# Value projection from rows instead of window columns, with its result sent through DRAM, and the bias product moved to the front of the projection

## The chip, the core and the metric

The kernel runs on one core of one Trainium2 chip. The metric is device time in microseconds (us), from the first to the last instruction and the few microseconds around them. Before the change three runs gave 4484.2, 4484.65 and 4484.88 us; the median is 4484.65 us.

A core has five engines that run side by side, each through its own list of instructions in order: TensorE (PE in the profile; PEld is its weight load), VectorE (DVE), ScalarE (ACT), GpSimd (POOL) and SyncE (SP), which here issues nearly all DMA transfers. Where one engine needs another's result, it waits on a semaphore.

## What is computed

The input is an image batch of shape 2 x 128 x 256 x 256 (batch, channel, row, column) in float32. One layer has two halves. The first is windowed attention with a halo: windows of 8 x 8 pixels ask, windows of 12 x 12 pixels answer, 4 heads of 32 channels. A fixed mask leaves, for each query, only keys of one parity of row and column. The second is a mixture of 8 experts, of which each pixel uses the best 2. Cut to what matters:

```
def conv(x):                        # x is normalised over the 128 channels
    q, k, v = split(W_qkv @ x)      # three 1x1 projections
    q = windows of 8x8 of q;  k, v = windows of 12x12 of k, v (zero padded)
    attn = softmax(q * SCALE @ k.T + rel_pos_emb(q * SCALE) + FIXED_MASK)
    return W_out @ (attn @ v)

def ffn(t):                         # t is normalised over the 128 channels
    p = softmax(t @ router_w);  top 2 of 8, weights scaled to sum 1
    return sum over the two of p_e * (t @ expert_w[e] + expert_b[e])

x = x + conv(ln(x));  x = x + ffn(ln(x))
```

## The kernel before

**Strips and planes.** The image is cut into 64 strips of 8 rows (two batch entries of 32). Because of the mask a query sees only pixels of its own row and column parity, so each strip falls into 4 planes (2 row parities x 2 column parities) of 4 rows by 128 columns. There are 256 planes, counted by `n`; `i, pl = divmod(n, 4)` gives the strip and the plane. In a plane a window has 4 x 4 queries and 6 x 6 keys. Two neighbouring windows are taken together: a pair has a patch of 6 rows by 10 columns, 60 places, padded to 64 (`KR, KC, NK, SLOT`). A plane has 16 pairs, two of which share one 128-row tile.

**The normalised rows.** `xn` (two buffers, one per strip parity) holds the normalised rows of a strip with its halo, channels on the partitions, with a zero column on both sides. `ln1` (L272) writes one row of `xn` per iteration on GpSimd; it needs the broadcast factor `rb`, which comes back from DRAM. `halo` (L246) copies the shared row on GpSimd, once in four iterations.

**Columns and values.** `columns` (L331) copies, on GpSimd, the new rows of `xn` into `xcol`: for each pair of windows the 64 places of its patch stand side by side. `place` (L251) gives a row's place in the ring of 6 rows, and `runs` (L255) groups rows whose places follow one another. `xcol` has one buffer per plane index `pl`, so that only new rows (4 of 6, as a rule) are copied. In `project`, `values` (L366) then runs 4 products of 128 x 128 by 128 x 128 (L369) with 128 columns of `xcol` as the weights, into one PSUM tile, and ScalarE copies that into `vv` (L376). It is called twice per plane: `values(0)` at the head of `project`, `values(4)` at its end. So the value of a pixel that lies in several patches is computed once for each patch.

**The other projections.** `pu` (L384) is the product for the relative position bias; VectorE transposes it into `uT` (L386), and `shift` makes two copies (L349) and one more transpose, `au` (L354). `pk` (L396) is the key projection from whole rows of `xn`; ScalarE spreads it into `kcol` (L407, L414). `pq` (L418) is the query projection; ScalarE copies it into `qs` (L420).

**PSUM.** `pvv`, `pu`, `pk`, `pq`, `plt`, `plg` and `po` all take their place from one pool of three buffers, `ps_mm`, in the order in which they are asked for. A tile can be written once the tile three before it has been read for the last time. Before the change the order in an iteration is `pvv`, `pu`, `pk`, `pq`, `plt`, `pvv`, `plg`, `po`.

**Attention.** `scores` (L448, L465) needs `au`, `kcol` and `qs`; ScalarE's Exp gives `pT` (L473). `attend` sums the weights with `ones` (L486) and multiplies with the values (L496); VectorE transposes the sums (`sT`, L506), inverts them (L508), spreads them (`rT`, L511) and scales the output (`o`, L516). `out_project` (L524) and the sum into `xt` (L529) end the attention of a plane.

**Experts.** For each row pair there are 8 gate tiles `gb`, fetched from DRAM by broadcast (L661). `times` (L677) multiplies the centred input `xs` by a gate into `xe`: VectorE does e = 0, 1, 2, 3, 4, 6, GpSimd e = 5, 7. `product` (L686) accumulates the 8 expert products in `acc`; `end` adds `acc` to `xt` (L692), and `store` writes it out.

**The order of the work** is written by hand: inside the main loop (L779 to L867) each engine keeps the order in which the lines are issued. Generators (`score`, `attn`, `ahead`, `norm` and others) are advanced by `next`. Iteration `n` runs the scores of plane `n`, then `ahead`, which is `project(n + 1)`, then expert products 4, 6, 7, 5 of the row before, the attention of plane `n`, expert products 0, 1, 2, the output projection and expert product 3. On VectorE the routing (L587 to L619) and the transpose of the gates, `gT` (L625), come ahead of `uT`; then come `shift`, `xs` (L671), six `times`, L692, L506 to L516, the transpose `plg` (L563), and `rstd`. On GpSimd a one-column copy, `behind` (L681), waits for VectorE's `xe` number 6; then follow `times(5)`, `ln1`, `halo`, `times(7)` and `columns`. PE's code is padded with empty instructions (L793) so that each iteration starts at the same place in a code block of 256.

**rstd** (L218) makes the reciprocal deviations from `plg`, which lies in PSUM:

```
mean, sq = (p4[:, :, E + 2 * k0 + j : E + 2 * k1 : 2].rearrange("p t k -> p k t") for j in range(2))
nc.vector.tensor_copy(r, mean)                                                  # L228
nc.vector.tensor_tensor(u, r, r, ALU.mult)                                      # L229
nc.vector.scalar_tensor_tensor(u, u, -1.0, sq, ALU.mult, ALU.add)               # L230
nc.vector.scalar_tensor_tensor(u, u, 0.0, epsc[:, k0:k1], ALU.max, ALU.add)     # L231
nc.scalar.activation(r, u, AF.Ln, scale=4.0)                                    # L232
```

`mean` and `sq` are views of PSUM; `r`, `u` and `epsc` lie in SBUF.

Of the kernel before, what the change touches and what calls it, by code (L numbers as in the profile page):

```python
# [11 lines left out]
F32 = mybir.dt.float32  # L12
AF = mybir.ActivationFunctionType
ALU = mybir.AluOpType
# [3 lines left out]
P = 128  # L18
# [33 lines left out]
def kernel(  # L52
# [42 lines left out]
    def ctile(shape, name):  # L95
        return const.tile(shape, F32, tag=name, name=name)
# [98 lines left out]
    nc.tensor.matmul(pr[:, :P], lhsT=wall[:, 0, :], rhs=relbd, start=True, stop=True)  # L195
    nc.vector.tensor_copy(wrel, pr[:, :P])

    xn, xcol, kcol = [], [], []
    for i in range(2):
        xn.append(ctile([P, 2, 2, KR, PC + 2], f"xn{i}"))  # L200
        nc.gpsimd.memset(xn[i][:, :, :, :, 0 : PC + 2 : PC + 1], 0.0)
    for i in range(4):
        xcol.append(ctile([P, HP, 2, SLOT], f"xcol{i}"))
        kcol.append(ctile([P, NP, SLOT], f"kcol{i}"))
        nc.gpsimd.memset(xcol[i][:, :, :, NK:], 0.0)
        nc.gpsimd.memset(kcol[i][:, :, NK:], 0.0)
        nc.gpsimd.memset(kcol[i][:, 0, 0:NK:KC], 0.0)
        nc.gpsimd.memset(kcol[i][:, NP - 1, KC - 1 : NK : KC], 0.0)
# [9 lines left out]
    def rstd(p4, k0, k1, name):  # L218

        u, r = (
            small.tile([P, 2, NT], F32, tag=v, name=f"{v}_{name}")[:, k0:k1] for v in ("u", "r")
        )
        mean, sq = (
            p4[:, :, E + 2 * k0 + j : E + 2 * k1 : 2].rearrange("p t k -> p k t") for j in range(2)
        )
        nc.vector.tensor_copy(r, mean)  # L228
        nc.vector.tensor_tensor(u, r, r, ALU.mult)  # L229
        nc.vector.scalar_tensor_tensor(u, u, -1.0, sq, ALU.mult, ALU.add)  # L230
        nc.vector.scalar_tensor_tensor(u, u, 0.0, epsc[:, k0:k1], ALU.max, ALU.add)  # L231
        nc.scalar.activation(r, u, AF.Ln, scale=4.0)  # L232
        nc.scalar.activation(r, r, AF.Exp, scale=-0.5)
        nc.vector.scalar_tensor_tensor(u, u, -4.0, r, ALU.mult, ALU.mult)
        nc.vector.tensor_tensor(u, u, r, ALU.mult)
        return r, u

    def ln_rows(i):

        s = strips[i][1]  # L240
        return range(1 if s == 0 else 2, KR - 1 if s == NS - 1 else KR)
# [13 lines left out]
    def runs(i, rows):  # L255

        out = []
        for k in rows:
            if out and place(i, k) == out[-1][1] + out[-1][2]:
                out[-1][2] += 1  # L260
            else:
                out.append([k, place(i, k), 1])
        return out
# [59 lines left out]
            ln1(i, k, pb, nc.vector)  # L323
        yield

    def columns(n):

        i, pl = divmod(n, 4)
        for k, at, m in runs(i, ln_rows(i)):
            for half in range(2):  # L330
                nc.gpsimd.tensor_copy(  # L331
                    xcol[pl][:, :, half, at * KC : (at + m) * KC].rearrange(
                        "p t (r c) -> p t r c", c=KC
                    ),
                    windows(xn[i % 2][:, pl // 2, pl % 2, k : k + m], half * HP, HP),
                )
        for k, s in ((0, 0), (KR - 1, NS - 1)):
            if strips[i][1] == s:
                c0 = place(i, k) * KC
                nc.gpsimd.memset(xcol[pl][:, :, :, c0 : c0 + KC], 0.0)  # L340
                nc.gpsimd.memset(kcol[pl][:, :, c0 : c0 + KC], 0.0)

    def shift(uT, n, state):

# [12 lines left out]
    def project(n, state):  # L357

        i, pl = divmod(n, 4)
        xp = xn[i % 2][:, pl // 2, pl % 2]  # L360
        inner = xp[:, 1 : 1 + PR, 1 : PC + 1]
        xl, kk = xcol[pl], kcol[pl]

        vv = work.tile([P, HP, P], F32, tag="vv", name=f"vv{n}")

        def values(t0):  # L366
            pv = mm_tile(f"pvv{n}_{t0}")
            for t in range(4):
                nc.tensor.matmul(  # L369
                    pv[:, t * P : (t + 1) * P],  # L370
                    lhsT=xl[:, t0 + t].rearrange("p a k -> p (a k)"),
                    rhs=wv,
                    start=True,
                    stop=True,
                )
            nc.scalar.copy(vv[:, t0 : t0 + 4, :].rearrange("p t c -> p (t c)"), pv)  # L376

        values(0)
        yield

        pu = mm_tile(f"pu{n}")
        nc.tensor.matmul(pu, lhsT=wrel, rhs=inner, start=True, stop=True)  # L384
        uT = work.tile([P, PR, 4, 32], F32, tag="uT", name=f"uT{n}", bufs=1)
        nc.vector.transpose(uT, pu.rearrange("p (a m s) -> p a s m", a=PR, s=4))  # L386
        state["shift"] = lambda: shift(uT, n, state)
        yield

        rows = list(ln_rows(i))  # L390
        for part in (rows[-4:], rows[:-4]):
            if not part:
                continue
            pk = mm_tile(f"pk{n}_{part[0]}")
            m = len(part)
            nc.tensor.matmul(  # L396
                pk[:, : m * PC],
                lhsT=wk,
                rhs=xp[:, part[0] : part[0] + m, 1 : PC + 1],
                start=True,  # L400
                stop=True,
            )
            pk3 = pk[:, : m * PC].rearrange("p (r c) -> p r c", r=m)
            for k, at, m in runs(i, part):
                new = pk3[:, k - part[0] : k - part[0] + m]
                places = kk[:, :, at * KC : (at + m) * KC].rearrange("p t (r c) -> p t r c", c=KC)
                nc.scalar.copy(places[:, 1 : NP - 1], windows(new[:, :, KC - 3 :], 0, NP - 2))  # L407

                ends = [places[:, 0, :, 1:], new[:, :, 0 : KC - 1]]
                for j, step in enumerate(((NP - 1) * SLOT - 1, PC - KC + 1)):  # L410
                    dims = [list(d) for d in ends[j].unsqueeze(1).ap]
                    dims[1] = [step, 2]
                    ends[j] = bass.AP(ends[j].tensor, ends[j].offset, dims)
                nc.scalar.copy(*ends)  # L414
        yield

        pq = mm_tile(f"pq{n}")
        nc.tensor.matmul(pq, lhsT=wq, rhs=inner, start=True, stop=True)  # L418
        qs = work.tile([P, 2 * NP, PR, 4], F32, tag="qs", name=f"qs{n}")
        nc.scalar.copy(  # L420
            qs.rearrange("p m a s -> p a m s"), pq.rearrange("p (a m s) -> p a m s", a=PR, s=4)
        )
        yield

        values(4)
        state.update(qs=qs, kk=kk, vv=vv)
        yield

    def windows(rows, n0, count):
# [315 lines left out]
            next(part)  # L745
    if len(strips) > 1:
        halo(1)
    columns(0)
    states = {0: {}}
    for _ in project(0, states[0]):  # L750
        pass
    states[0]["shift"]()
    if n_planes > 1:
        columns(1)

# [20 lines left out]
    with tc.manual_schedule(engines={ET.PE, ET.DVE, ET.Activation, ET.Pool, ET.SP}):  # L778
        for n in range(n_planes + 7):  # L779
# [32 lines left out]
            next(ahead, None)  # L812
            if n + 1 < n_planes:
                states[n + 1]["shift"]()
            next(ahead, None)
            next(ahead, None)
            for e in (4, 6, 7, 5):
# [26 lines left out]
            new.fetch(3, dve)  # L844
            while to_store:
                store(*to_store.pop())
            next(ahead, None)
            ex.product(0)
            made = next(norm, None)
# [8 lines left out]
                halo(i + 2)  # L858
            nxt.times(7, pool)
            if n + 2 < n_planes:  # L860
                columns(n + 2)
            next(outp, None)
            ex.product(3)
            next(outp, None)
# [61 lines left out]
```

The softmax here doesn't subtract the row's maximum and nothing guards it: scores larger than these inputs give would overflow.

## Time and profile before

| What | Value |
|---|---|
| three runs | 4484.2, 4484.65, 4484.88 us |
| span of the profiled execution | 4480.1 us (the median run stands 4.55 us above it) |
| mean granted clock of TensorE | 0.997 |
| a usual iteration (from one uT to the next) | 17.16 us |
| ScalarE's and GpSimd's share of the span | 33% and 29% |
| transfer of one gate tile, issue to landing | 4.0 us median, 256 KB |
| write of the gates to DRAM, issue to landing | 3.0 us median, 16 KB |
| transfers issued per iteration | 8 gb, 1 sb, 1 rb, 2 gd, 1 xt, 1 output |

No separate time is listed for the profiled execution; its span is set beside the median of the runs. The page says for every engine how long it was busy, and for the costliest lines how long one instruction took ("mean ns of one"), how long the engine sat idle just before it, and what ended that idle time. A float32 product on PE shows as two instructions; L369's x4096 is 2048 products. The timeline gives start and duration of instructions; overlapping neighbours on PE are pipelined, so the cost of a step is read from one start to the next.

### The profile page before, as it was taken

The numbers are of one execution on the slowest core, as the hardware profiler recorded it, in microseconds if no ns is written. First come the engines' busy times: TensorE is split into PE (matmuls) and PEld (weight loads), VectorE is DVE, ScalarE is ACT, GpSimd is POOL, SyncE is SP. The second block draws the span as 40 slices with busy tenths as digits, with TensorE's granted clock in tenths as the row PEclk, the third lists the DMA queues.
The fourth block names the chain that finished last, engine by engine and source line by source line (L and its number), as shares of the span: only waits on it lengthen the run. The fifth ranks groups of instructions, "written<-read, shape, count | busy, mean of one in ns | idle before, by whom it ended". The sixth has DMA issues, their size and how long they took to land. (4 is left out here: it accounts for less than half of the span.)

```text
span 4480.1 us, 224632 instructions
## 1 busy us (share of the span) xinstructions
PE 4422.6 (99%) x96321; PEld 2683.3 (60%) x96321; DVE 3996.2 (89%) x11850; ACT 1467.7 (33%) x4022; POOL 1317.7 (29%) x1815
## 2 busy tenths in 40 slices
PE   7999999999999999999999999999999999999997
PEld 5666666666666666666666666666666666666653
DVE  5899999999899999998989999999999999989887
ACT  3333333333333333333333333333333333333321
POOL 1232323232323233232323232323232323232321
PEclk9999999999999999999999999999999999999999
DMA  2565666566656666666666566666665666566655
GB/s 83 174 191 185 192 185 192 186 191 185 193 184 192 185 191 187 189 188 188 189 187 189 187 190 185 193 183 193 184 193 185 192 185 192 186 191 186 190 164 186
DMA packets 519284, 828.12 MB, mean 185 GB/s; under 512 B 124186, under 2 KB 125850, under 8 KB 518298
## 3 DMA queue, kind: packets, MB, share of 16 engines
q1 hardware_dynamic: 517568, 813.46, 58.3%
q8 instruction: 769, 12.60, 1.1%
q14 instruction: 217, 1.78, 0.2%
q10 hardware_dynamic: 730, 0.29, 0.0%
HBM read 737.95 MB, written 75.56 MB: 182 GB/s over the span
## 5 line engine op out<-in xcount | busy, mean ns | idle before, releaser
L686 PE MATMUL acc<-xe,ew 128*128 128x512 f32 x4096 | 1889.0, 594 | 19.6 <-DVE gb L660 18.8
L686 PEld LDWEIGHTS acc<-xe,ew 128*128 128x128 f32 x4096 | 758.8, 190 | 885.7 <-issue 861.8
L677 DVE TENSOR_TENSOR xe<-xs,gb 128x512 f32<-128x512 f32 x1536 | 950.9, 687 | 10.2 <-PE acc L686 0.7
L681 POOL COPY last<-xe 128x1 f32<-128x1 f32 x256 | 47.9, 187 | 3060.8 <-DVE gb L660 3054.6
L376 ACT COPY vv<-pvv 128x512 f32<-128x512 f32 x512 | 299.8, 586 | 1395.7 <-PE pvv L369 1379.6
L677 POOL TENSOR_TENSOR xe<-xs,gb 128x512 f32<-128x512 f32 x512 | 650.8, 1272 | 5.9 <-PE att L496 2.5
L369 PE MATMUL pvv<-wt,xcol 128*128 128x128 f32 x4096 | 594.3, 288 | 2.5 <-POOL xcol L331 1.5
L369 PEld LDWEIGHTS pvv<-wt,xcol 128*128 128x128 f32 x4096 | 496.4, 191 | 64.8 <-issue 51.8
L272 POOL TENSOR_TENSOR xn<-xt,rb 128x512 f32<-128x512 f32 x249 | 375.0, 1506 | 66.5 <-DMA rb<-gd 55.9
L465 PE MATMUL att<-qs,kcol 32*64 32x32 f32 x32768 | 392.4, 226 | 0.8 <-issue 0.7
L465 PEld LDWEIGHTS att<-qs,kcol 32*64 32x64 f32 x32768 | 391.0, 130 | 1.0 <-issue 1.0
L496 PEld LDWEIGHTS att<-pT,vv 64*32 64x32 f32 x32768 | 348.0, 105 | 39.4 <-issue 2.5
L496 PE MATMUL att<-pT,vv 64*32 64x32 f32 x32768 | 343.2, 200 | 2.3 <-issue 2.3
L473 ACT ACTIVATE pT<-att 128x1024 f32<-128x1024 f32 x256 | 261.9, 1023 | 243.1 <-PE att L465 239.7
L548 ACT ACTIVATE sq<-xt 128x512 f32<-128x512 f32 x505 | 292.7, 631 | 0.0
L354 DVE STREAM_TRANSPOSE au<-auT 128x512 f32<-128x512 f32 x256 | 269.2, 1052 | 9.0
L524 PE MATMUL po<-o,wt 128*128 128x512 f32 x512 | 262.0, 593 | 6.1 <-DVE o L516 3.2
L384 PE MATMUL pu<-xn,wrel 128*128 128x512 f32 x512 | 262.5, 594 | 0.0
L407 ACT COPY kcol<-pk 128x560 f32<-128x560 f32 (+2 forms) x344 | 174.1, 506 | 268.2 <-PE pk L396 265.3
L418 PE MATMUL pq<-xn,wt 128*128 128x512 f32 x512 | 262.0, 593 | 0.0
L396 PE MATMUL pk<-xn,wt 128*128 128x512 f32 (+2 forms) x528 | 261.0, 578 | 0.0
L386 DVE STREAM_TRANSPOSE uT<-pu 128x512 f32<-128x512 f32 x256 | 182.8, 714 | 78.0 <-PE pu L384 77.0
(2697 smaller groups left out, 5243.8 us busy)
## 6 DMA issues: line engine op xcount, KB each, us to landing
gb<-gd SPq DMA_DIRECT2D x2048, 256.0 KB, 4.0
xt<-in_x_dram SPq DMA_DIRECT2D x256, 256.0 KB, 4.9
sb<-gd SPq DMA_DIRECT2D x256, 256.0 KB, 3.5
out_dram<-xt SPq DMA_DIRECT2D x256, 256.0 KB, 4.2
rb<-gd SPq DMA_DIRECT2D x249, 256.0 KB, 3.3
gd<-gT SPq DMA_DIRECT2D x516, 16.0 KB, 3.0
ew<-in_L_ffn_expert_w_dram SPq DMA_DIRECT2D x1, 512.0 KB, 5.0
eb<-in_L_ffn_expert_b_dram SPq DMA_DIRECT2D x1, 512.0 KB, 5.7
```

The lines of the kernel that those rows point to most:

```text
L272: eng.tensor_tensor(xn[i % 2][:, :, :, k, 1 : PC + 1], ln1_src(i, k).rearrange("p (y j x) -> p y x j", y=2, x=2), rb.rearrange("p (y j x) ...
L354: nc.vector.transpose(au.rearrange("p m a s -> p a s m"), auT[n % 2])
L369: nc.tensor.matmul(pv[:, t * P : (t + 1) * P], lhsT=xl[:, t0 + t].rearrange("p a k -> p (a k)"), rhs=wv, start=True, stop=True,)
L376: nc.scalar.copy(vv[:, t0 : t0 + 4, :].rearrange("p t c -> p (t c)"), pv)
L384: nc.tensor.matmul(pu, lhsT=wrel, rhs=inner, start=True, stop=True)
L418: nc.tensor.matmul(pq, lhsT=wq, rhs=inner, start=True, stop=True)
L465: nc.tensor.matmul(sc[rows, h, 32 * t : 32 * t + 32], lhsT=kk[hp, half * HP + t, :], rhs=qs[hp, m0 : m0 + 2].rearrange("p m a s -> p (m a ...
L496: nc.tensor.matmul(av[hp, half, 32 * t : 32 * t + 32], lhsT=vv[rows, t, hp], rhs=pT[rows, h, 32 * t : 32 * t + 32], start=True, stop=True,)
L524: nc.tensor.matmul(po, lhsT=wo, rhs=state["o"].rearrange("p f z -> p (f z)"), start=True, stop=True)
L548: nc.scalar.activation(sq, src, AF.Square)
L677: eng.tensor_tensor(self.xe[e], self.xs, self.gb.pop(e), ALU.mult)
L686: nc.tensor.matmul(self.acc, lhsT=ew[:, e, :], rhs=self.xe.pop(e), start=(e == 0), stop=not self.xe)
```

## The change

The value projection no longer works on window columns. `xcol`, `columns`, `values` and the tile `vv` go. In their place:

- `value_rows(n)` runs one 128 x 128 by 128 x 128 product per new row of the plane (4 as a rule; 5 for the first strip of an image, 3 for the last), with the row's 128 columns as the weights, into `pv`, and ScalarE copies the result into `vr`: image columns on the partitions.
- `send_values` writes `vr` to a DRAM buffer, `vrows` (one per `pl`, 6 ring rows of 130 columns of 128 channels), in one or two transfers of 256 KB together.
- `take_values` reads the windows back into `vwin` (one per `pl`): for each ring row (4 as a rule, 6 for the first strip of an image) and each half one transfer of 10 columns x 8 pairs x 128 channels, each run 512 bytes, with 10 destination partitions.
- `borders` replaces `columns`: at the top and bottom strip it clears `kcol`'s row and writes a zero row into `vrows`.

In the hand-written order `pu` comes first in `project`, with the row products right behind it, and then a `yield`; VectorE's transpose of `pu` is issued in the next part. `send_values` follows `shift`, ahead of `fetch_means`; `take_values` follows the store, ahead of `fetch(4)`. The order of PSUM tiles in an iteration becomes `pu`, `pv`, `pk`, `pq`, `plt`, `plg`, `po`; the tile three before `pq` is then `pu`. In `rstd`, L229 multiplies `r` by `mean` and no longer by itself.

```
-        nc.vector.tensor_tensor(u, r, r, ALU.mult)
+        nc.vector.tensor_tensor(u, r, mean, ALU.mult)
...
+    def value_rows(n):
+        i, pl = divmod(n, 4)
+        xp = xn[i % 2][:, pl // 2, pl % 2]
+        rows, sent = list(ln_rows(i)), []
+        for part in (rows[-4:], rows[:-4]):
+            if not part:
+                continue
+            pv = mm_tile(f"pv{n}_{part[0]}")
+            m = len(part)
+            for j, k in enumerate(part):
+                nc.tensor.matmul(pv[:, j * P : (j + 1) * P], lhsT=xp[:, k, 1 : PC + 1], rhs=wv, start=True, stop=True)
+            vr = work.tile([P, 4, P], F32, tag="vr", name=f"vr{n}_{part[0]}")
+            nc.scalar.copy(vr[:, 0:m].rearrange("p r c -> p (r c)"), pv[:, : m * P])
+            sent.append((part, vr))
+        return sent
+    def send_values(n, sent):
+        i, pl = divmod(n, 4)
+        for part, vr in sent:
+            for k, at, m in runs(i, part):
+                nc.sync.dma_start(
+                    vrows[pl][at : at + m, 1 : PC + 1, :].rearrange("r c d -> c r d"),
+                    vr[:, k - part[0] : k - part[0] + m],
+                )
+    def take_values(n):
+        i, pl = divmod(n, 4)
+        s = strips[i][1]
+        for k in range(0 if s == 0 else 2, KR):
+            at = place(i, k)
+            for half in range(2):
+                p0 = half * SLOT + at * KC
+                src = vrows[pl][at, half * HP * 8 : half * HP * 8 + KC, :].unsqueeze(1)
+                dims = [list(d) for d in src.ap]
+                dims[1] = [8 * P, HP]
+                nc.sync.dma_start(vwin[pl][p0 : p0 + KC], bass.AP(src.tensor, src.offset, dims))
...
-        values(0)
-        yield
         pu = mm_tile(f"pu{n}")
         nc.tensor.matmul(pu, lhsT=wrel, rhs=inner, start=True, stop=True)
+        state["sent"] = value_rows(n)
+        yield
+
         uT = work.tile([P, PR, 4, 32], F32, tag="uT", name=f"uT{n}", bufs=1)
         nc.vector.transpose(uT, pu.rearrange("p (a m s) -> p a s m", a=PR, s=4))
...
-        values(4)
-        state.update(qs=qs, kk=kk, vv=vv)
+        state.update(qs=qs, kk=kk, vv=vwin[pl])
...
                 states[n + 1]["shift"]()
+                send_values(n + 1, states[n + 1]["sent"])
...
                 store(*to_store.pop())
+            if n + 1 < n_planes:
+                take_values(n + 1)
...
             if n + 2 < n_planes:
-                columns(n + 2)
+                borders(n + 2)
```

Ahead of the loop, `vwin` and the side columns of `vrows` are cleared, and plane 0 is projected, sent and taken.

## The prediction

> **What bounds the kernel now.** I read the page's busy shares first, then its costliest groups, then the timeline of one usual iteration, last the waits.
>
> ```profile
> PE 4422.6 (99%) x96321; PEld 2683.3 (60%) x96321; DVE 3996.2 (89%) x11850; ACT 1467.7 (33%) x4022; POOL 1317.7 (29%) x1815
> ...
> L369 PE MATMUL pvv<-wt,xcol 128*128 128x128 f32 x4096 | 594.3, 288 | 2.5 <-POOL xcol L331 1.5
> ...
> L386 DVE STREAM_TRANSPOSE uT<-pu 128x512 f32<-128x512 f32 x256 | 182.8, 714 | 78.0 <-PE pu L384 77.0
> ```
>
> PE is busy throughout and VectorE nearly so. VectorE's only large wait for PE is uT's for pu. The timeline of one iteration (start, duration) shows the places that the change touches:
>
> ```profile
> 2003.39 1.16 PE L369 MATMUL pvv<-wt,xcol 128*128 128x128 f32 x8
> ...
> 2004.39 1.02 PE L384 MATMUL pu<-xn,wrel 128*128 128x512 f32 x2
> ...
> 2005.25 1.02 PE L396 MATMUL pk<-xn,wt 128*128 128x512 f32 x2
> ...
> 2005.45 0.72 DVE L386 STREAM_TRANSPOSE uT<-pu 128x512 f32<-128x512 f32 x1
> ...
> 2006.11 1.02 PE L418 MATMUL pq<-xn,wt 128*128 128x512 f32 x2
> ...
> 2010.95 1.34 PE L496 MATMUL att<-pT,vv 64*32 64x32 f32 x128
> ...
> 2012.43 0.71 DVE L506 STREAM_TRANSPOSE sT<-att 128x512 f32<-128x512 f32 x1
> ...
> 2014.93 1.27 POOL L677 TENSOR_TENSOR xe<-xs,gb 128x512 f32<-128x512 f32 x1
> ...
> 2015.39 0.83 DVE L229 TENSOR_TENSOR u__116_37779<-r__116_37780 128x8 f32<-128x8 f32 x1
> ...
> 2016.14 1.10 POOL L331 COPY xcol<-xn 128x160 f32<-128x160 f32 x4
> ...
> 2016.45 0.29 DVE L231 SCALAR_TENSOR_TENSOR u__116_37779<-u__116_37779,epsc 128x8 f32<-128x8 f32 x1
> ```
>
> The thing to see is L229: 8 elements take 0.83 us, and it ends at 2016.22, 0.02 after GpSimd's product. In the first iterations, with GpSimd idle, the same line takes 0.16 us. So an operation of VectorE with both inputs in SBUF stands still until GpSimd's instruction ends. L230, with one input in PSUM, takes 0.16 always. L231 (u and epsc, both SBUF) takes 0.29 here and 0.42 in iterations whose column copies end later: it waits too.
>
> VectorE is therefore a second bound just below PE. Over the 243 loops from the 13th on (one uT to the next) I summed the records: loop 17.169 us, of which uT's wait for pu 0.218 and the waits of L506 and L529 for PE 0.047. Without those VectorE would need 16.90.
>
> **Part 1: the products.** A block of four value products costs PE 1.00 us from start to start (2003.39 to 2004.39). Two such blocks become one: PE's own loop falls from 17.16 to 16.16. The other PE steps stay. ScalarE has one copy of 0.59 us less, at 33% busy: nothing. GpSimd loses the column copies, 1.10 us behind its last product: nothing by themselves, since no PE line waits for xcol (2.5 us in all).
>
> **Part 2: L229.** With mean in PSUM, L229 should take 0.17. The stall does not vanish, L231 inherits it: it is ready 0.40 us after L229's start (0.17 + 0.16 + two gaps of 0.035) and then waits for GpSimd's product, which ends 0.90 us after that start on average over these loops. L231 so ends at 0.92; now it ends at 0.90 + 0.04 + 0.16 + 0.04 + 0.23 = 1.35. The same sum loop by loop gives 0.425. Bounds: 0 if reading PSUM twice brings a new wait, 0.86 if L231 did not wait (it did in the copies' rows, so 0.425).
>
> [...]
>
> **Part 3: the order.** pu comes one block earlier, so uT no longer waits for it: 0.218. In exchange pq waits for uT. Now pq starts at 2006.11 and uT ends at 2006.17. With VectorE as the slower engine, PE reaches pq first and stands until uT's end. A product that stood for VectorE is shown once, po for o in the first plane: o ends at 43.44, po starts at 43.59 and its pair takes 1.10, not 1.02; 0.23 in all. So pq counts as started at 2006.40, 0.29 later against uT than now. Queued behind it on PE: products 4, 6, 7, 5, the attention, plt. Who waits for those: L692 needs acc at 2011.82 and would have it at 2010.85; L506 would start at 2012.29 + 0.29 + 0.11 (the latency in loops where it waited) = 2012.69, not 2012.43: VectorE loses 0.26 there. But GpSimd's chain (last, product 5, ln1, product 7) starts from xe number 6, ahead of L506, and VectorE waits for its end at L231 anyway, 0.50 on average and 0.40 at least in usual loops. The 0.26 comes out of that wait and costs nothing. If that cover is gone, every further 0.1 us costs 24 us. L506's and L529's waits (0.047) go, because po comes earlier against VectorE.
>
> **Part 4: the transfers.** SP gets 8 reads and 1 or 2 writes more, about 0.35 us of issue each (0.32 to 0.56 in its rows): 14 transfers by 0.35 are 4.9 us of a loop now, 8.4 after. send_values stands behind rb, which waits for the gates' write, and ahead of sb, which is used a loop later. take_values waits for the write's landing (issued near 2009.1, 3 to 5 us by the rows), is issued from 2015.7 to about 2018.5 and pushes fetch(4) and fetch(6) some 2.8 us later; their gates land at about 2023 and 2024 and are used after 2027. gd of the next loop is issued after 2022. vwin is there by 2023, attend reads it at about 2027. PE must wait for up to 8 transfers; its semaphore instruction takes 0.051 us, 0.41 in all, in the sequencer, which runs ahead while products 4, 6, 7, 5 take 3.5 us: nothing.
>
> DMA load:
>
> ```profile
> q1 hardware_dynamic: 517568, 813.46, 58.3%
> ```
>
> That is 0.583 of 16 engines; in a usual iteration 10.5 of 17.16 us. Added are 512 packets out and 640 in, 512 bytes each. If each of the ten destination partitions keeps to one engine, ten engines get 32 + 64 = 96 packets per loop, else all get 72. The trace's packet records have 512-byte packets in the start-up loads: 29.6 ns mean. 1536 bytes take 68, 2048 bytes 103 under load. I take 29.6: 10.5 + 2.8 = 13.3 of 16.5 us, no bound. Both ends: 72 x 0.027 = 1.9 and 96 x 0.103 = 9.9 us.
>
> [...]
>
> **The sum.** 0.218 + 0.047 + 0.425 = 0.690 us per loop; 16.48 remains, above PE's 16.16. Times 243: 167.7 us. The first twelve loops and the tail I leave as they are, and add 3 us for plane 0's way through DRAM (write 4, twelve issues by 0.35, landing 4, against values ready before its attention at 39.5). 4480.1 - 167.7 + 3 = 4315.4; the median stands 4.55 above the span: **4320 us**. About 0.2% is what a measurement here can tell from no change.
>
> **Rivals.**
> 1. *The forecast* (VectorE behind GpSimd bounds): 4280 to 4350, as the cover holds wholly and start-up gains, or 0.1 us of it is missing.
> 2. *pq's wait takes the gain's place.* If PE restarts later, or waits for vwin in the open (0.41), the cover of 0.40 is passed by some 0.3: 0.3 x 243 = 73, 4393 us; from 4350 to 4430, where Part 2 gives nothing (0.425 x 243 = 103). For it: pq stands directly behind uT. Against: the spare 0.14 and the sequencer running ahead.
> 3. *PE bounds.* L231 does not wait, VectorE needs 16.05, PE 16.16 and some restarts: 1.0 x 243 = 243, 4242 us; 4230 to 4280. Against it: L231's 0.42.
> 4. *Slower: the DMA engines bound.* It decides when a packet costs more than (17.17 - 10.5) / 96 = 69 ns, on ten engines. At 84 ns, the lower quartile of the 2048-byte packets, the loop is 18.6: 4485 + 1.4 x 243 = 4825 us. Against: 29.6 ns.
> 5. *It doesn't do what it says*: pq never waits, as PE is the later engine. Then PE's loop is the longer, which needs rival 3; counted there.
>
> **How the numbers follow.** Chances: forecast 0.63, rival 2 0.19, rival 3 0.08, rival 4 0.10. The forecast with rival 2 holds 0.82: range 4280 to 4430. Faster by over 0.2%: 0.63 + 0.19 + 0.08, less 0.01 for a rival 2 that eats all: 0.89; within 0.2%: 0.02, that and the edge of rival 4; slower: 0.09.
>
> **What would show it.** Right: loops of about 16.4 us, every fourth about 16.75; uT's wait for pu gone; L229 at 0.17 and L231 near 0.5 after GpSimd's product; a wait of pq for uT; L506 waiting some 0.2 us for PE. Wrong: VectorE idle over 0.5 us ahead of L506 (rival 2); L231 at 0.17 throughout and PE without gaps (rival 3); PE waiting for vwin or GpSimd for rb, with new packets over 69 ns (rival 4). What I can't see is how PE restarts behind a wait in every loop, and packets of 512 bytes under load.

## The result and the profile after

The changed kernel takes 5191.61 us (median of four runs, 5159.85 to 5253.7) against 4484.42 us: ratio 1.156, interval 1.151 to 1.161. The forecast was 4320 us. So the change costs 707 us, or about 3 us in each of the 243 usual loops: a loop from one uT to the next is now 20.24 us on average, before it was 17.17. The profiled execution is the longest of the four, 5253.7 us with a span of 5251.8 and a mean granted TensorE clock of 0.925; the other three stand at 0.932 to 0.935, and what is read below from the changed kernel's trace is of the longest.

The edit moves the lines: L229 to L231 of before are now L233 to L235, uT is L416, pq L448, the values of the attention L525, sT L535, ln1 L276, and SyncE's transfers are L690 (gates `gb`), L662 (`gd`), L666 (`rb`), L369 (the write of the value rows) and L385 (their reads). First the page of the changed kernel: busy time, costliest groups, and the DMA queue.

```profile
PE 4563.1 (87%) x94273; PEld 2605.9 (50%) x94273; DVE 4008.5 (76%) x11850; ACT 1310.8 (25%) x3774; POOL 1092.5 (21%) x1128
...
q1 hardware_dynamic: 843720, 966.94, 62.0%
...
L525 PE MATMUL att<-pT,vwin 64*32 64x32 f32 x32768 | 372.4, 203 | 477.8 <-issue 477.4
...
L535 DVE STREAM_TRANSPOSE sT<-att 128x512 f32<-128x512 f32 x256 | 183.5, 717 | 548.9 <-PE att L525 548.1
L276 POOL TENSOR_TENSOR xn<-xt,rb 128x512 f32<-128x512 f32 x249 | 373.3, 1499 | 575.7 <-DMA rb<-gd 540.1
...
L448 PE MATMUL pq<-xn,wt 128*128 128x512 f32 x512 | 280.6, 630 | 130.0 <-DVE uT L416 129.7
```

PE is no longer busy throughout: 87%, not 99%. Four idle times are new or far longer. PE stands 478 us at the products with `vwin`, VectorE stands 548 us behind them (11 before), GpSimd stands 540 us for `rb` ahead of ln1 (56 before), and pq stands 130 us for uT (0 before). The DMA engines are no fuller than 62%. So waiting has entered the loop, not an engine's work. The same four lines in the kernel before:

```profile
L272 POOL TENSOR_TENSOR xn<-xt,rb 128x512 f32<-128x512 f32 x249 | 375.0, 1506 | 66.5 <-DMA rb<-gd 55.9 <-ACT qs L420 10.5
...
L496 PE MATMUL att<-pT,vv 64*32 64x32 f32 x32768 | 343.2, 200 | 2.3 <-issue 2.3
...
L418 PE MATMUL pq<-xn,wt 128*128 128x512 f32 x512 | 262.0, 593 | 0.0
...
L506 DVE STREAM_TRANSPOSE sT<-att 128x512 f32<-128x512 f32 x256 | 182.2, 712 | 11.4 <-PE att L496 10.6 <-issue 0.5
```

The first of the four is easily misread. It looks as if PE waited for `vwin`, but the page names no releaser ("issue"). The view of line L525 says what ended the idle time of its matmuls and weight loads together (us, times), and the timeline of a loop in which PE stood says where it lies:

```profile
  issue: 969.2, 286
  DMA vwin<-vrows: 0.8, 2
```

```profile
2682.21 1.12 PE L525 MATMUL att<-pT,vwin 64*32 64x32 f32 x103
2686.10 0.44 PE L525 MATMUL att<-pT,vwin 64*32 64x32 f32 x25 [2.77 <-issue]
```

PE stood 0.8 us for `vwin` in the whole run. It begins with the values on time, does 103 of a plane's 128 products and only then stands. Of its 143 idle times over 0.3 us at this line, 141 lie at the 104th or 106th product; and of the 150 in the usual loops for which the profile names nothing, at whatever line, 147 end 1.0 to 1.9 us (1.4 in the median) after the end of one of the 16 KB packets of queue q8, kind "instruction". I take these packets for PE's code by a count: the trace has 769 of them and 196,955 instructions of TensorE, 256 to a packet, as many as the code block to which the kernel pads. So I read these idle times as stalls for PE's own code, and not for `vwin`; the experiments below come back to it.

One iteration of the changed kernel (start, duration, in brackets the idle time before it) shows the other waits:

```profile
2002.38 1.49 POOL L276 TENSOR_TENSOR xn<-xt,rb 128x512 f32<-128x512 f32 x1 [3.16 <-DMA rb<-gd]
...
2002.74 0.16 DVE L233 TENSOR_TENSOR u__100_32711<-r__100_32712,plg 128x8 f32<-128x8 f32 x1
...
2003.13 0.77 DVE L235 SCALAR_TENSOR_TENSOR u__100_32711<-u__100_32711,epsc 128x8 f32<-128x8 f32 x1
...
2004.42 5.69 SPq L385 DMA_DIRECT2D vwin<-vrows  x8
...
2009.89 0.67 DVE L416 STREAM_TRANSPOSE uT<-pu 128x512 f32<-128x512 f32 x1
...
2010.22 2.03 SPq L690 DMA_DIRECT2D gb<-gd  x4
...
2010.62 1.13 PE L448 MATMUL pq<-xn,wt 128*128 128x512 f32 x2 [0.74 <-DVE uT L416]
...
2012.35 1.18 SPq L662 DMA_DIRECT2D gd<-gT  x2
...
2017.20 0.33 SPq L666 DMA_DIRECT2D rb<-gd  x1
...
2020.63 1.50 POOL L276 TENSOR_TENSOR xn<-xt,rb 128x512 f32<-128x512 f32 x1 [2.62 <-DMA rb<-gd]
...
2021.08 1.07 DVE L238 SCALAR_TENSOR_TENSOR u__101_33034<-u__101_33034,r__101_33035 128x8 f32<-128x8 f32 x1 [0.52 <-ACT r__101_33035 L237]
```

What the forecast said of VectorE is there: L233 takes 0.16, L235 inherits the wait. But read SyncE's rows (SPq). The eight reads take 5.69 us to issue, not 2.8. Behind them stand four gate fetches and then `gd`. uT starts at 2009.89, directly behind gT, so `gd` could go at 2009.9; it goes at 2012.35. `rb` follows at 2017.20 and ln1 at 2020.63, some 10.7 us behind uT; the mean is 10.4, and 8.0 in the kernel before. There ln1 is so late that it runs beside L238 and L239: VectorE's L238 takes 1.07 instead of 0.17. On average L238 and L239 take 0.47 us a loop longer than in the kernel before, more than Part 2 won.

What does SyncE wait for between two reads? Its waits in the changed kernel (line, what it waited for: us in total, times, longest):

```profile
SPq L666 <- DMA gd<-gT: 677.6, 249, 4.6
SPq L385 <- DMA gb<-gd: 484.9, 750, 2.4
...
SPq L385 <- DMA xt<-in_x_dram: 97.8, 187, 1.8
SPq L385 <- DMA out_dram<-xt: 66.9, 189, 1.7
SPq L385 <- DMA sb<-gd: 59.1, 115, 1.4
```

and in the kernel before, where the wait of `rb` for `gd` is the only large one for a landing, and no transfer waits for a place in the usual loops (the second row's four are at the start):

```profile
SPq L637 <- DMA gd<-gT: 457.2, 249, 3.2
...
SPq L115 <- DMA xt<-in_x_dram: 2.8, 4, 1.4
```

A read of `vwin` needs nothing from a gate tile, an input row or an output. Yet the reads wait 709 us (484.9 + 97.8 + 66.9 + 59.1) for such landings. The records explain it: every transfer raises one semaphore when it lands, and these run from 101 to 108 and round again, in the order in which the kernel issues its transfers. The eight reads of one iteration, from the records (issued at, waits for semaphores, raises semaphore):

```
1304.06  105 110  105
1305.04  106 110  106
1306.31  107      107
1307.00  108      108
1307.63  101      101
1308.32  102      102
1308.95  103      103
1309.61  104      104
```

Each waits for the very semaphore that it will raise itself. (110 is PE's, which has to be done with the tile. The place of the first read, 105, was that of the write of the rows, issued at 1299.02, eight places before it.) So a transfer is issued only when the one eight places before it has landed. I call this **theory Q** (the queue's eight places). These waits stand in the program's own instructions; whether the chip could hold more transfers in flight, no run shows.

The count is simple. In the kernel before 14 transfers of some 4 us landing share a loop of 17.17: 14 x 4 / 17.17 = 3.3 places are taken on average. Now 23.4 transfers share it. By the records a gate tile lands in 5.1 us (median), an input row in 7.2, a read of `vwin` in 3.1; the landing times add up to 104 us a loop, 104 / 20.24 = 5.2 places of 8. That is the mean; behind the store, where eight reads follow fetches and stores closely, the eight run out.

The rivals that I tested against Q: **W**, pq's wait for uT (the order); **B**, the bytes and packets of the reads (the DMA engines).

### The profile page after: what moved, and what is told of

Its sections match the earlier page's. It is cut to its first block, busy times and chain, and to the rows that moved or that the text cites. A ratio compares the mean times of both kernels' runs of the same rounds, so it can differ in the third digit from the quotient of the medians.

```text
span 5251.8 us, 226268 instructions
## 1 busy us (share of the span) xinstructions
PE 4563.1 (87%) x94273; PEld 2605.9 (50%) x94273; DVE 4008.5 (76%) x11850; ACT 1310.8 (25%) x3774; POOL 1092.5 (21%) x1128
## 5 line engine op out<-in xcount | busy, mean ns | idle before, releaser
L715 PE MATMUL acc<-xe,ew 128*128 128x512 f32 x4096 | 2113.3, 652 | 25.1 <-DVE gb L689 21.3
L715 PEld LDWEIGHTS acc<-xe,ew 128*128 128x128 f32 x4096 | 839.7, 211 | 1085.8 <-issue 1027.4
L525 PE MATMUL att<-pT,vwin 64*32 64x32 f32 x32768 | 372.4, 203 | 477.8 <-issue 477.4
L525 PEld LDWEIGHTS att<-pT,vwin 64*32 64x32 f32 x32768 | 359.0, 107 | 531.1 <-issue 491.9
L535 DVE STREAM_TRANSPOSE sT<-att 128x512 f32<-128x512 f32 x256 | 183.5, 717 | 548.9 <-PE att L525 548.1
L276 POOL TENSOR_TENSOR xn<-xt,rb 128x512 f32<-128x512 f32 x249 | 373.3, 1499 | 575.7 <-DMA rb<-gd 540.1
L448 PE MATMUL pq<-xn,wt 128*128 128x512 f32 x512 | 280.6, 630 | 130.0 <-DVE uT L416 129.7
L350 PEld LDWEIGHTS pv<-wt,xn 128*128 128x128 f32 x2048 | 268.5, 191 | 127.5 <-issue 64.7
L558 DVE TENSOR_TENSOR xt<-po,xt 128x512 f32<-128x512 f32 x256 | 176.2, 688 | 199.1 <-PE po L553 198.9
L411 PE MATMUL pu<-xn,wrel 128*128 128x512 f32 x512 | 290.0, 648 | 0.0
L621 ACT ACTIVATE lg<-lg 128x32 f32<-128x32 f32 x256 | 58.7, 229 | 857.8 <-DVE lg L620 857.8
L350 PE MATMUL pv<-wt,xn 128*128 128x128 f32 x2048 | 270.9, 275 | 1.2 <-DVE uT L416 1.0
```

What stands on the lines that cost most here:

```text
L276: eng.tensor_tensor(xn[i % 2][:, :, :, k, 1 : PC + 1], ln1_src(i, k).rearrange("p (y j x) -> p y x j", y=2, x=2), rb.rearrange("p (y j x) ...
L350: nc.tensor.matmul(pv[:, j * P : (j + 1) * P], lhsT=xp[:, k, 1 : PC + 1], rhs=wv, start=True, stop=True,)
L525: nc.tensor.matmul(av[hp, half, 32 * t : 32 * t + 32], lhsT=vv[rows, t, hp], rhs=pT[rows, h, 32 * t : 32 * t + 32], start=True, stop=True,)
L715: nc.tensor.matmul(self.acc, lhsT=ew[:, e, :], rhs=self.xe.pop(e), start=(e == 0), stop=not self.xe)
```

## The experiments

Means per loop, over the loops from the 13th on, in us, are worked out from the records:

| kernel | time | loop | end of gT to `gd` | uT to ln1 | PE idle in all | of it at the products with the values | behind a code packet |
|---|---|---|---|---|---|---|---|
| before | 4484 | 17.17 | 0.47 | 7.99 | 0.01 | 0 | 0 |
| mean_only | 4481 | 17.16 | 0.54 | 8.00 | 0.01 | 0 | 0 |
| after | 5192 | 20.24 | 2.65 | 10.40 | 2.52 | 1.92 | 1.93 |
| rows_first | 5222 | 20.09 | 2.45 | 10.46 | 2.45 | 2.15 | 2.37 |
| take_thin | 5175 | 19.63 | 2.74 | 10.73 | 2.12 | 1.41 | 1.42 |
| two_takes | 4705 | 17.96 | 1.30 | 9.65 | 1.26 | 0.12 | 0.69 |
| no_take | 4454 | 17.03 | 1.34 | 8.60 | 0.51 | 0 | 0.25 |
| before_reads | 4765 | 18.29 | 2.50 | 10.52 | 0.66 | 0.14 | 0.19 |
| reads_act | 4492 | 17.19 | 0.47 | 7.99 | 0.02 | 0 | 0.01 |
| take_act | 5194 | 19.93 | 0.06 | 7.91 | 2.39 | 0.05 | 0.06 |
| take_pool | 5682 | 21.96 | 1.38 | 8.34 | 3.58 | 3.51 | 3.53 |
| two_takes_pool | 4816 | 18.43 | 1.54 | 9.45 | 1.66 | 0.04 | 1.34 |
| ahead | 4393 | 16.72 | 0.11 | 8.37 | 0.34 | 0.23 | 0.23 |
| ahead_late | 4482 | 17.08 | 0.32 | 8.47 | 0.60 | 0.52 | 0.51 |

The last column sums PE's idle times of over 0.3 us for which the profile names nothing and which end 1.0 to 1.9 us after the end of a code packet. It overlaps with the column before it.

**mean_only**: the kernel before with the one edit in rstd.

```
-        nc.vector.tensor_tensor(u, r, r, ALU.mult)
+        nc.vector.tensor_tensor(u, r, mean, ALU.mult)
```

> The kernel before with L229's edit alone (u = r * mean). All theories: PE still needs 17.16 us per loop, so 4470 to 4486 us. L229 at 0.17 us, L231 longer (about 0.5), since GpSimd's product still holds it. If L231 stays at 0.2, the inheritance of the stall that the prediction took is wrong.

4481.07 us; ratio 0.9991, interval 0.9982 to 1.0001. L229 and L231 together fall from 1.137 to 0.712 us a loop, by the 0.425 that was forecast; 0.12 of it is given back at L234 and L235. The loop stays at 17.16, for PE bounds it: uT's and L529's waits for PE grow from 0.28 to 0.55. So this edit alone buys nothing and harms nothing.

**rows_first**: the changed kernel with the row products ahead of pu, so that pu is no longer the tile three before pq.

```
+        state["sent"] = value_rows(n)
         pu = mm_tile(f"pu{n}")
         nc.tensor.matmul(pu, lhsT=wrel, rhs=inner, start=True, stop=True)
-        state["sent"] = value_rows(n)
```

> The changed kernel with the row products ahead of the bias product, so that pq takes the PSUM place of pv and no longer that of pu. Theory Q (queue: SyncE issues a transfer only when the one eight before it has landed, and the eight reads of take_values fill all eight places): 5100 to 5250 us, little changed. Rival W (pq's wait for uT, 270 us of PE idle in the trace of after): below 4950 us. Rival B (bytes on ten DMA engines): 5100 to 5250, little changed.

5222.37 us; ratio 1.165, 1.161 to 1.168. pq's idle time falls from 0.52 to 0.01 a loop and nothing is won. W falls. PE's idle time behind code packets is longer there (2.37).

**take_thin**: each read brings 8 of 128 channels; the rest of `vwin` stays zero.

```
-                src = vrows[pl][at, half * HP * 8 : half * HP * 8 + KC, :].unsqueeze(1)
+                src = vrows[pl][at, half * HP * 8 : half * HP * 8 + KC, 0:8].unsqueeze(1)
```

> The changed kernel, but each read of take_values brings 8 of 128 channels (runs of 32 bytes for 512): same number of transfers, same waits, a sixteenth of their bytes; the other channels of vwin stay zero. Theory Q: 4900 to 5200 us, since the number of transfers in the rotation counts and not their size. Rival B: 4300 to 4400 us, as the ten engines are relieved. Rival W: 5150 to 5250.

5174.77 us (5107 to 5268), as long as the changed kernel with a sixteenth of the bytes read. So the bytes are not the cost. The number of packets is the same here; that more packets can go with less time is shown by the next run.

**two_takes**: DRAM and window places are ordered by column and row, so that a half's 60 places are one run of rows and each plane needs two reads of 60 partitions, not eight of 10; all six ring rows are read.

```
-                src = vrows[pl][at, half * HP * 8 : half * HP * 8 + KC, :].unsqueeze(1)
...
+        for half in range(2):
+            src = vrows[pl][half * HP * 8 : half * HP * 8 + KC].rearrange("c r d -> (c r) d")
```

> The changed kernel with vrows held column by column and the patch places in that order too (column, row), so that take_values needs 2 reads of 60 destination partitions for 8 of 10, and the write has runs of 2 KB. All six ring rows are read: 960 packets of 512 bytes for 640, half as many bytes more; 17 to 18 transfers per loop for 23 to 24. Theory Q: 4300 to 4400 us, near the prediction's sum. Rival B: 5150 us or more. Rival W: 5100 to 5250.

4704.74 us; ratio 1.050, 1.047 to 1.053: 487 us less, with half as many bytes and packets again read. B falls. Six transfers fewer, and the largest part of the loss is gone. It is no gain yet, and Q's forecast of 4300 to 4400 was missed. GpSimd still waits for `rb`, and PE's stalls behind code packets are fewer and lie elsewhere, most of them at the expert products (idle time behind the second bar):

```profile
L712 PE MATMUL acc<-xe,ew 128*128 128x512 f32 x4096 | 1947.3, 603 | 118.2 <-issue 101.9 <-DVE gb L686 14.8 <-DVE xt L718 0.9
```

PE waits for nothing that the profile names ("issue"). There are 187 such stalls of over 0.3 us in the usual loops, 181 us in all, nearly all at the 96th recorded instruction behind the padding, counted modulo 256; 182 end 1.0 to 1.9 us after the end of a code packet. The kernel before has three, none behind a code packet. The code comes in 16 KB packets, three a loop. The page counts them, as it does the transfers' packets, as a share of the 16 DMA engines, which are busy 14.0 us of 17.96 here (10.4 of 17.17 before). That PE stands for the next code block is what I read from these times; no run moved the code to test it. The load is not enough to explain it: in the changed kernel and in take_pool, with more of this idle time, the engines are less busy (12.9 us of 20.24 in the first, q1 at 55.0% of the span in the second), and ahead below, with 13.5 of 16.72, has little of it.

**before_reads**: the reverse. The kernel before, with eight reads of 2.5 KB behind the store, into tiles that nobody uses.

```
+            if n + 1 < n_planes:
+                thin_reads(n + 1)
```

> The kernel before, whole, with eight small reads added per loop behind the store on SyncE's queue: 10 partitions x 8 runs of 32 bytes, from a DRAM buffer into tiles that nothing uses. Theory Q: the rotation alone slows it, 4600 to 5000 us. Rival B: 4484 to 4500 us, since the reads carry 20 KB per loop in all.

4765.38 us; ratio 1.062, 1.060 to 1.064. Nothing of the change is in it but eight transfers, and `gd` is about as late as in the changed kernel (2.50). The waits of SyncE are of the same kind:

```profile
SPq L659 <- DMA gd<-gT: 795.8, 249, 4.6
SPq L229 <- DMA gb<-gd: 638.4, 936, 2.4
SPq L229 <- DMA out_dram<-xt: 154.6, 205, 1.8
SPq L229 <- DMA xt<-in_x_dram: 88.4, 234, 0.7
```

What makes the loop longer can be seen here alone, as PE stands only 0.66 us a loop. ln1 begins 2.5 us later, GpSimd's work then runs beside other lines of VectorE, and VectorE's instructions take 18.13 us a loop and not 16.96: 1.17 more, in a loop that is 1.12 longer. The waits for places make 881 us (638.4 + 154.6 + 88.4), 3.4 a loop, and `gd` comes 2.0 later than in the kernel before. What the eight issues (some 0.3 us each) would do without such waits, no run shows by itself.

**reads_act** and **take_act** ask whom the eight places belong to: the same reads as in before_reads, and the reads of the changed kernel, issued by ScalarE.

```
-                nc.sync.dma_start(
+                nc.scalar.dma_start(
```

> As before_reads (the kernel before with eight small reads of 2.5 KB per iteration behind the store, into tiles that nobody uses), but issued by ScalarE and no longer by SyncE. Theory Q, first form (a transfer waits for the eighth before it among those of the same issuing engine): SyncE has its old list of 14 transfers again, its waits for gb, xt and output landings go, gd and rb are issued as in the kernel before, and the time comes close to the kernel before: 4485 to 4560. Second form (the eight places are shared by both issuing engines): the time stays by that of before_reads, 4700 to 4800. Rival (eight more transfers cost their time in the DMA engines, whoever issues them): also 4700 to 4800, but with SyncE free of waits for landings and with longer landings of gb.

> The changed kernel with take_values issued by ScalarE, at the same place of the order; nothing else differs. ScalarE has some 7 us without work between its two squares and the next plane's rstd, so the eight issues find room. Theory Q, first form (places counted per issuing engine): SyncE's list is fetches, gd, rb, writes as before, so gd and rb come on time; what remains is what the kernel without reads and the two-read kernel show, longer landings and code loads of TensorE: 4500 to 4680. Second form (places shared): SyncE still stands for landings, 5000 to 5250. Rival (the bytes and packets of the reads are the cost): 5000 to 5250 without SyncE's waits.

reads_act: 4491.54 us, ratio 1.0009 (1.0 to 1.0019). take_act: 5194.42 us, ratio 1.157 (1.154 to 1.161). My two forms of Q give opposite answers here, and the trace of take_act settles it: the transfers of both issuers raise semaphores 101 to 108, and each issuer waits for the other's, so the places are shared. (GpSimd's reads in take_pool have a set of their own, 111 to 118.) SyncE waits for ScalarE's reads, at its gate fetches:

```profile
SPq L690 <- DMA vwin<-vrows: 527.3, 242, 6.5
```

and ScalarE, having the reads in its list, stands for SyncE's transfers. The timeline of take_act:

```profile
2016.83 7.44 ACTq L385 DMA_DIRECT2D vwin<-vrows  x8
...
2020.22 0.35 DVE L235 SCALAR_TENSOR_TENSOR u__101_33034<-u__101_33034,epsc 128x8 f32<-128x8 f32 x1
2024.31 0.21 ACT L236 ACTIVATE r__101_33035<-u__101_33034 128x8 f32<-128x8 f32 x1 [12.63 <-DMA vwin<-vrows]
...
2024.79 0.17 DVE L238 SCALAR_TENSOR_TENSOR u__101_33034<-u__101_33034,r__101_33035 128x8 f32<-128x8 f32 x1 [4.22 <-ACT r__101_33035 L237]
```

SyncE's urgent transfers are on time (`gd` 0.06 behind gT, ln1 without a wait), but rstd's logarithm stands behind the reads, and VectorE idles 4.10 us a loop at L238, before 0.515. The wait has changed its engine and the time is the same, yet PE's idle time behind code packets is gone (0.06, with the same products in the same order): the equal times are a coincidence of two different losses. In reads_act the places are shared too, so the second form of Q missed its time by some 200 us: there the reads wait for no write and nothing urgent stands behind them on ScalarE, and SyncE's waits for places (565 us for gate tiles and for ScalarE's reads) leave `gd` where it was, 0.47 behind gT.

The times alone give no answer as to whether the issuer matters: take_act takes 5194 us against the changed kernel's 5192, while the same eight small reads cost 280 us from SyncE (before_reads) and some 4 from ScalarE (reads_act). What the traces add is that SyncE and ScalarE share eight places here, and that what stands behind the waits on the issuer's list decides.

**take_pool** and **two_takes_pool**: the eight, and the two, reads issued by GpSimd behind its `times(7)`.

> The changed kernel with the same eight reads per loop, of the same size, issued from GpSimd's queue behind its last product, no longer from SyncE's. Theory Q: SyncE's rotation holds only 15 to 16 transfers per loop again, so 4300 to 4450 us, with GpSimd's own issue time as the unknown. Rival B (bytes, ten engines, small packets): 5100 us or more, as the DMA engines do the same work.

> The kernel with two reads (column order), these two issued from GpSimd's queue. Theory Q: 4300 to 4400 us, at or below the run with eight reads from that queue. If the DMA engines' load is what kept two_takes at 4705, as its longer landings may say (gate tiles 6.6 us for 4.0), 4600 to 4720.

5682.22 us (ratio 1.267, 1.265 to 1.270) and 4815.51 us (1.073, 1.072 to 1.075). Both expectations missed. SyncE's waits for places go in take_pool and ln1 is nearly on time (8.34 behind uT), and yet it is the slowest of all, by PE's stalls:

```profile
PE att L525 <- issue: 871.0, 227, 6.3
```

PE stands 3.51 us a loop there, again not for `vwin`: 223 of the 227 idle times lie at the 104th or 106th product, and the reads have landed 8.5 us before the first (median). Nearly all of it ends behind a code packet (3.53 in the table). This run speaks against the places as the whole cause: SyncE waits for none, and the reads still cost more than in the changed kernel. Of two_takes_pool's loop, 1.34 us are stalls behind code packets, and ln1 still waits 1.24 us for `rb`.

**no_take**: the rows are written to DRAM and never read; `vwin` stays zero.

```
-            if n + 1 < n_planes:
-                take_values(n + 1)
```

> The changed kernel without the reads of take_values: vwin stays zero, the values are still computed and written to DRAM. Theory Q: 4300 to 4400 us, the prediction's sum without its part 4. If it stays above 4500, the write or the order costs, too.

4454.04 us; ratio 0.9925, 0.9902 to 0.9947, over what I expected. VectorE's instructions take 16.55 us of the loop of 17.03, and 16.96 of 17.17 in the kernel before: 0.41 less, where 0.425 was forecast for L229 and L231, so VectorE's gain was sized well. The other 0.48 of the loop is waiting: a gate tile lands in 5.9 us and not in 4.0, ln1 waits 0.67 for `rb`, and 87 unnamed stalls of PE cost 74.5 us. Even without the reads the round trip takes most of the gain. With the reads the time is 738 us longer, and PE's idle time behind code packets goes from 0.25 to 1.93 us a loop: the reads bring it.

**ahead** and **ahead_late**: two reads, and the whole value path one plane earlier. The row products of plane n + 2 stand behind expert product 3 and are written at the end of the iteration; in ahead the reads of plane n + 1 stand between `gd` and `rb`, where SyncE waits for `gd`'s landing anyway. ahead_late has them behind the store, as the change does.

```
+            sent = value_rows(n + 2) if n + 2 < n_planes else []
...
+            if n + 2 < n_planes:
+                send_values(n + 2, sent)
```

> Two reads (column order), and the whole value path one plane earlier: row products of plane n + 2 behind expert product 3, write at the loop's end, the two reads of plane n + 1 between the gates' write (gd) and rb, where SyncE only waits for gd's landing. pq's place in PSUM is then free of uT's wait. Theory Q: SyncE's waits for the rotation and ln1's wait for rb shrink: 4330 to 4430 us, below the kernel before. If PE's code loads (idle at code positions 96, 352 and 608 of a loop, 148 times in two_takes) follow from the DMA engines' load of 14 us per loop, they stay: 4450 to 4600 us.

> As ahead, but with the two reads behind the store, where the changed kernel has them. It parts the place on SyncE's queue from the lateness of vwin: theory Q expects the fetches, gd and rb to be pushed back as in two_takes, 4600 to 4700 us; if the time of two_takes came from vwin's lateness or from pq's wait, it is as fast as ahead.

ahead: 4392.62 us, ratio 0.978 (0.9761 to 0.9799), faster than both kernels. ahead_late: 4481.66 us, 0.9989 (0.9978 to 0.9999); I had expected 4600 to 4700, with `gd` pushed back as in two_takes, but it is only 0.32 behind gT. So the earlier path is worth some 223 us against two_takes (4705 to 4482), and the place of two reads on SyncE's list another 89. SyncE's wait for the landing of `gd`, ahead of `rb`, in ahead and then in ahead_late:

```profile
SPq L663 <- DMA gd<-gT: 137.1, 221, 2.6
```

```profile
SPq L663 <- DMA gd<-gT: 740.0, 249, 4.4
```

The reads have moved into that wait. And the page of ahead has PE busy again:

```profile
PE 4235.1 (96%) x94273; PEld 2512.2 (57%) x94273; DVE 3903.2 (89%) x11850; ACT 1444.4 (33%) x3774; POOL 1094.6 (25%) x1128
...
q1 hardware_dynamic: 822864, 1007.52, 77.6%
```

with the DMA engines fuller (77.6%) than in the changed kernel (62.0%). Their mean load alone doesn't make the loss.

## Why the prediction was wrong

**What bounds, Part 1, Part 2: right in kind.** PE's busy part of the loop falls from 17.16 to 16.38 us in ahead (16.72 less 0.34; forecast 16.16), VectorE's instructions by 0.41 in no_take (forecast 0.425). L229 (now L233) fell to 0.16, L231 (now L235) inherited the wait, and their sum fell by 0.425 in mean_only. I overlooked 0.12 at L234 and L235, which meet GpSimd's next instruction.

**Part 3: right in kind, beside the point.** uT's wait for pu fell from 77 us in the kernel before to 24. pq waits for uT. Its cover was passed (0.52 a loop), but removing that wait wins nothing (rows_first).

**Part 4 is the step that failed.** It put the eight reads at 0.35 us of SyncE's issue each, and all that they touch in a usual loop at nothing. Without them the time is 4454 us, with them 5192. Two terms were missing.

The first is the places. I priced a transfer on SyncE by its issue alone and took issue to depend on nothing. But in this program a transfer also takes one of eight places (semaphores 101 to 108) until it has landed. The eight reads needed 5.69 us of SyncE in the loop above, not 2.8. I looked at what they push, found fetch(4) and fetch(6) used much later, and put `gd` "after 2022", clear of them; I did not follow the list on to `rb`. `gd` comes 2.65 us behind gT, `rb` and ln1 follow late, and VectorE's lines meet GpSimd. before_reads shows this chain by itself: 280 us.

The second, as I read it, is PE's code, for which there was no term at all: 1.93 us of PE's idle time a loop lie behind code packets. That the reads bring it is shown by no_take (0.25), and that they need not, by take_act (0.06); why the packets come late in these loops stays open. In the loops with a stall the packet starts 1.9 us after the first product with the values (median), in the others 3.1 us before it, and in the kernel before 2.8 us before it; the packet itself takes some 0.95 us in all three. What Part 4 said of `vwin` held: it is there ahead of the attention, and PE's waits for its eight transfers cost nothing (0.8 us in the run).

How the 3.07 us between the loops of the kernel before (17.17) and the changed one (20.24) divide can be read from VectorE. Its instructions take as long as before (16.96): what L229 won is lost again at lines that meet GpSimd. Its waits grow: 2.13 for the attention, in whose products PE stands 1.92 behind code packets, 0.74 for `po`, 0.35 for gate tiles; uT's falls by 0.21. The wait for `po` fits PE's clock: PE's busy time is 4563 us against 4267 in no_take with the same products, 296 / 256 = 1.16 a loop. Products are slower in the stages that the trace shows at half clock: 1061 ns against 592 for an instruction of the expert products (below).

**The rivals.** Rival 4 had the right sign and the wrong cause. It asked for packets of over 69 ns; the 512-byte packets take 27.8 on average, near the 29.6 that I took, and the DMA engines' load rose by 2.5 us a loop, forecast 2.8. Rival 2's wait came, and taking it away won nothing. One rival on the slower side that I should have had stood in the same profile: the issue rows of SyncE, counted as transfers in flight. No run shows the ten engines that the 96 packets of Part 4 and of rival 4's 69 ns suppose, nor an even deal: the records don't name the engine of a packet, and what the runs show is the load above, a mean over 16.

## What to carry to other kernels

Count transfers in flight, not only bytes and issue time, and count them where they crowd: transfers times landing time, over the stretch, against the places there are (here eight, by the semaphores). The mean over the loop does not rank the kernels (5.2 places in the changed one, 5.9 in two_takes, 5.0 in ahead). Then walk the issuing engine's list behind each added transfer, to its end and around the loop, to the first one that somebody waits for at once. Here a round trip through DRAM paid only in few transfers, started a plane earlier, and issued where the issuing engine stands anyway (ahead). And where the profile names nothing for an idle time, see at which instruction of the line it lies before naming a cause, and look at the code packets.

## What I had not expected of the hardware

- **Eight places, shared by SyncE and ScalarE.** 20 KB a loop in eight reads cost 6.2% when SyncE issues them (before_reads) and nothing that can be told from noise when ScalarE does (reads_act, ratio 1.0009). The limit stands in the program's semaphores, 101 to 108.
- **PE stood, as I read the times, for its own code.** In the changed kernel 147 idle times, 468 us in all, end 1.0 to 1.9 us after the end of a code packet (in take_pool 234, 859 us; in the kernel before none). It was not a matter of the DMA engines' mean load (above).
- **Half clock began at idle times of a few us.** By the clock records of the changed kernel's trace, a stage at half clock began during PE's idle time or within 3.5 us behind it in 2 of 97 cases when the idle time was 0.3 to 1.8 us, in 11 of 19 at 1.8 to 2.1, in 65 of 75 at 2.1 to 3, and in 84 of 85 over 3 us. In take_act it was 51 of 63 at 2.1 to 3 us. By 20 us windows of the changed kernel (length, PE, PEld, DVE, ACT, POOL busy, then granted clock, DMA share and GB/s):

```profile
2240.00:2260.00 20.00, 15.56 (x363) 9.14 (x362) 15.31 (x47) 4.97 (x14) 4.91 (x6) 0.88 0.74 203
...
2280.00:2300.00 20.00, 17.67 (x391) 9.76 (x397) 15.97 (x54) 5.40 (x17) 4.71 (x5) 1.00 0.72 212
```

In the stages at half clock an instruction of the expert products (L715) took 1061 ns (median of 338), outside them 592 (median of 3758).

- **Landing times differed, and not by the bytes alone.** A gate tile lands in 4.0 us in the kernel before and in 5.9 in no_take, with 256 KB more written a loop. But it also lands in 5.5 us in before_reads, with 20 KB read and nothing written, and in 4.2 when ScalarE issues the same reads (reads_act). The write's own part in no_take isn't separated.
